# The graph stage by pairs of blocks: scores and attention in two-bank tiles

## The chip, the cores and the metric

The kernel runs on one core of one Trainium2 chip. The metric is the device time of one execution in microseconds; 2288.53 us is the median of three runs of the kernel before (2284.22 to 2291.29). Five engines work beside each other, each through its own queue in order: TensorE (matmuls, PE in the profile, its weight loads PEld), VectorE (DVE), ScalarE (ACT), GpSimd (POOL) and SyncE (SP), which issues the DMA transfers. Engines wait for one another by semaphores.

## The reference

The module is one decoder layer of three parts: a graph feature stage on `x`, a gated state-space scan, and a low-rank feed-forward part. Only the first concerns the change. For each batch of 512 nodes it orders the nodes along four space-filling curves, takes for each node and curve a window of ten neighbours, and runs a small attention over the ten:

```python
        def _get_graph_features(feats, inds_list, perm, W_lin, b_lin, k=K):
            ...
            for inds in inds_list:
                neigh = gather(feats, inds)
                gf = jnp.concatenate([jnp.broadcast_to(center, (B, N, k, C)), neigh - center], axis=-1)
                per_method.append(gf)
            allf = jnp.stack(per_method, axis=-1)
            allf = allf[..., perm]
            total = 2 * C * M_METHODS
            x = allf.reshape(B * N, k, total)
            x16 = x.astype(jnp.float16).astype(jnp.float32)
            ...
            scores = jnp.einsum('bihd,bjhd->bhij', qh, qh) / np.float32(np.sqrt(headdim))
            attn = jax.nn.softmax(scores, axis=-1)
            out = jnp.einsum('bhij,bjhd->bihd', attn, qh).reshape(B * N, k, total)
            fused = out @ W_lin.T + b_lin
            return fused.reshape(B, N, k, 64)
        ...
        g1 = _get_graph_features(f0, inds_list, perm1, W_lin1, b_lin1)
        h1 = jnp.einsum('oc,bnkc->bonk', W_conv1, g1)
        h1 = _lrelu(_instance_norm(h1, (2, 3)))
        feats1 = h1.max(axis=-1)
        g2 = _get_graph_features(feats1.transpose(0, 2, 1), inds_list, perm2, W_lin2, b_lin2)
        h2 = jnp.einsum('oc,bnkc->bonk', W_conv2, g2)
        h2 = _lrelu(_instance_norm(h2, (2, 3)))
        feats2 = h2.max(axis=-1)
```

## The kernel before

**Passes and blocks.** The sixteen batches are worked on in four groups of four. Each group goes through layer 1 (32 output channels, `npair` 1) and layer 2 (64, `npair` 2), which makes eight passes, in the order of `order` (L1026): layer 1 of groups 0 and 1, layer 2 of 0, layer 1 of 2, layer 2 of 1, layer 1 of 3, layer 2 of 2 and of 3. A pass is cut into 43 blocks of twelve nodes (`NGRP`, `NG`), so there are 344 blocks. The stage is written under a manual schedule: each engine's queue has the instructions in the order of the program text.

**One block.** `differences` (L782, GpSimd) subtracts centres from neighbours into `DD`, and every third block SyncE spreads a piece of three blocks from `DD` to `DX` (L821, four transfers). `scores` (L841, TensorE) lays a mask of large numbers into a PSUM tile `s` of one bank (L846) and adds sixteen small matmuls (L853). `greatest` (L860, VectorE) takes the negative maximum `c` of each row of scores. `expo` (L867) adds `c` to `s` by a matmul (L870, TensorE) and takes the exponential `e` (L875, ScalarE). `sums` (L878, VectorE) adds `e` up to `z`. `shares` (L885) has the reciprocal `rz` on VectorE (L888) and the product `EN` = `e` x `rz` on GpSimd (L890). `turn` (L892, VectorE) transposes 32 x 32 blocks of `EN` to `e2`. `mapped` (L899) projects the differences to `u` with 48 matmuls (L915, TensorE), which ScalarE copies to `us` (L920; one copy of 512 columns in layer 1, two in layer 2). `outputs` (L923) multiplies `us` with `e2` into `h` (L943, sixteen fp32 matmuls; four blocks share an `h` tile in layer 1, two in layer 2). When an `h` tile is full, `reduce` (L950, VectorE) adds the centre's share in layer 2 (`hs`, L960), takes the maximum over the ten neighbours (L966) and the statistics for the norm (L969); in layer 2 a part of it is put off by one block (`rest`, L981).

**Beside it.** `prep` (L627) is a generator that prepares the next pass: a layer norm or a transpose, one-hot matrices `oh` on VectorE (L751), and `place` (L701), twelve matmuls on TensorE that permute the features (L705). `steps` (L1045) moves it on by one or two steps for each block, or moves a tail, the closing work of the pass before. `rank_step` (L551) compares sort keys, one matmul (L540) and one ScalarE instruction (L541) at a time, to find the nodes' order for the later groups.

**The order.** The loop over blocks (L1074) starts each part at its own distance behind the newest block `it`: `scores`, `greatest` and `mapped` at 0, `expo`, `sums` and `shares` at 1, `turn` and `outputs` at 3, `reduce` at 4, `rest` at 5; `differences` runs six blocks ahead (`LEAD`). The score tiles have two buffers (`ps_s`, L611), `EN` has two tiles (L442). PSUM is full: two banks of `s`, two of `u`, two for `misc`, one for `pp`, one for `h`.

Of the kernel before, what the change touches and what calls it, by code (L numbers as in the profile page):

```python
# [18 lines left out]
P = 128  # L19
B = 16  # L20
C = 32
D = 512
# [355 lines left out]
def graph_part(nc, tc, cx, I, dram, id32, ones, xt, F0, layernorm_steps, rstd_steps, scan_input):  # L378
# [63 lines left out]
    EN = [keep.tile([P, NI, 32], F32, name=f"EN{k}") for k in range(2)]  # L442
# [32 lines left out]
    for t in (*DD, *EN):  # L475
        zero(t)
# [134 lines left out]
    ps_s = cx.enter_context(tc.tile_pool(name="gps_s", bufs=2, space=PSUM))  # L611
# [3 lines left out]
    def early_tile(n):  # L615
        if n % 2:
            return ps_s.tile([P, 512], F32, tag="s", name=f"kd{n}")
        return later_tile(n)
# [222 lines left out]
    def scores(at, gi):  # L841

        slot, c1 = at_piece(at, gi)
        d, dx = DD[slot], DX[slot]
        s = ps_s.tile([P, 512], F32, tag="s", name=f"s{at}_{gi}")[:, :NI * QB]
        nc.tensor.matmul(  # L846
            s, lhsT=mL.rearrange("p i q -> p (i q)"), rhs=mR, start=True, stop=False, skip_group_check=True
        )
        for j in range(NJ):
            c0 = c1 + j * QB  # L850
            for h in range(4):
                rh = slice(32 * h, 32 * h + 32)
                nc.tensor.matmul(  # L853
                    s[rh, j * 4 * QB:(j + 1) * 4 * QB].rearrange("p (b q) -> p b q", b=4),
                    lhsT=d[:, h, c0:c0 + 32], rhs=dx[:, h, :, c0:c0 + QB],
                    start=False, stop=(j == NJ - 1), skip_group_check=True,
                )
        live["s", at, gi] = s

    def greatest(at, gi):  # L860
        c = sm.tile([P, NI], BF16, tag="c", name=f"c{at}_{gi}")
        nc.vector.tensor_reduce(  # L862
            c, live["s", at, gi].rearrange("p (i q) -> p i q", q=QB), AX.X, ALU.max, negate=True
        )
        live["c", at, gi] = c

    def expo(at, gi):  # L867

        s, c = live.pop(("s", at, gi)), live.pop(("c", at, gi))
        nc.tensor.matmul(  # L870
            s, lhsT=idb, rhs=c.unsqueeze(2).to_broadcast([P, NI, QB]), start=False, stop=True,
            skip_group_check=True,
        )
        e = sm.tile([P, NI, QB], F32, tag="e1", name=f"e1{at}_{gi}", bufs=3)
        nc.scalar.activation(e, s.rearrange("p (i q) -> p i q", q=QB), AF.Exp, scale=smc)  # L875
        live["e1", at, gi] = e

    def sums(at, gi):  # L878

        e = live.pop(("e1", at, gi))  # L880
        z = sm.tile([P, NI], F32, tag="z", name=f"z{at}_{gi}")
        nc.vector.tensor_reduce(z, e, AX.X, ALU.add)  # L882
        live["z", at, gi] = e, z

    def shares(at, gi):  # L885
        e, z = live.pop(("z", at, gi))
        rz = sm.tile([P, NI], F32, tag="rz", name=f"rz{at}_{gi}")
        nc.vector.reciprocal(rz, z)  # L888
        en = EN[(at * NGRP + gi) % 2]
        nc.gpsimd.tensor_tensor(en[:, :, :QB], e, rz.unsqueeze(2).to_broadcast([P, NI, QB]), ALU.mult)  # L890

    def turn(at, gi):  # L892

        e = sm.tile([P, NI, 32], F32, tag="e2", name=f"e2{at}_{gi}", bufs=2)
        en = EN[(at * NGRP + gi) % 2]
        nc.vector.transpose(e.rearrange("p i q -> p (i q)"), en.rearrange("p i q -> p (i q)"))  # L896
        live["e2", at, gi] = e
# [25 lines left out]
    def outputs(at, gi):  # L923
        key, co, npair, WA, hc, per = state[at][:6]
        us, e = live.pop(("us", at, gi)), live.pop(("e2", at, gi))
        slot = gi % per
        if slot == 0:
            live["h", at] = ps_1.tile([P, npair, per * NQ], F32, tag="h", name=f"h{at}_{gi}")
            if npair == 1:

                f0 = gi * NG
                nn = min(f0 + per * NG, D) - f0
                nc.tensor.matmul(
                    live["h", at][:, 0, :nn * K].rearrange("p (n j) -> p n j", j=K), lhsT=id32,
                    rhs=hc[:, 0, f0:f0 + nn].unsqueeze(2).to_broadcast([P, nn, K]), start=True, stop=False,
                    skip_group_check=True,
                )
        h = live["h", at]
        for j in range(NJ):
            for b in range(4):  # L940
                pr, r = divmod(b * co, P)
                q0 = slot * NQ + j * QB
                nc.tensor.matmul(  # L943
                    h[r:r + co, pr, q0:q0 + QB], lhsT=us[:, j, b * co:(b + 1) * co],
                    rhs=e[:, 4 * j + b, :QB], start=npair > 1, stop=True, skip_group_check=True,
                )
        if slot == per - 1 or gi == NGRP - 1:
            live["full", at, gi] = h

    def reduce(at, gi):  # L950
# [14 lines left out]
        def greatest_of():  # L965
            nc.vector.tensor_reduce(mxo[:, :, f0:f0 + nn], hs, AX.X, ALU.max)  # L966

        def moments(pr):
            nc.vector.bn_stats(stats[:, pr, gi // per], hs[:, pr].rearrange("p n j -> p (n j)"))  # L969

        if npair == 1:
            greatest_of()
            moments(0)
        else:
            moments(0)
            live["rest", at] = lambda: (greatest_of(), moments(1))
        if gi == NGRP - 1:
            rest(at, gi)
            tails.append(end(at))

    def rest(at, gi):  # L981
        if ("rest", at) in live:
            live.pop(("rest", at))()
# [27 lines left out]
    def finish(g, F2):  # L1011
# [6 lines left out]
        n3 = wk.tile([P, D], F32, tag="n3", name=f"n3_{g}", bufs=1)  # L1018
# [55 lines left out]
    for it in range(len(blocks) + 5):  # L1074

        def do(step, lag):
            if 0 <= it - lag < len(blocks):
                step(*blocks[it - lag])

        at, gi = blocks[it] if it < len(blocks) else (len(order), 0)  # L1080
        if gi == 0 and it < len(blocks):
            begin(at)
        do(expo, 1)
        for oh, of in transfers:
            nc.scalar.dma_start(out=oh, in_=of)
        transfers.clear()
        do(turn, 3)
        do(scores, 0)
        do(rest, 5)
        do(reduce, 4)  # L1090
        if ranked[0] < wanted(at):
            rank_step(later_tile)
        do(greatest, 0)
        do(mapped, 0)
        do(sums, 1)
        if at + 1 == len(order) and gi == 4:
            tails.extend(scan_input(sm, junk(q), q) for q in range(NBG - 1))
        steps(at, gi)
        do(shares, 1)
        if ranked[0] < wanted(at) and (at == 0 or gi % 2):  # L1100
            rank_step(later_tile)
        do(outputs, 3)
        if at == 0 and gi < 8:
            rank_step(later_tile)
        if it + LEAD < len(blocks):
            to, g2 = blocks[it + LEAD]
            if g2 == 0:
                for _ in ahead[to][0]:
                    pass
            differences(to, g2)  # L1110
# [563 lines left out]
```

## Time and profile before

| what | us |
|---|---|
| median of three runs | 2288.53 (2284.22 to 2291.29) |
| the profiled execution, whole time | 2296.19 |
| the profiled execution, span from first to last instruction | 2294.1 |
| TensorE busy, in the whole span | 2099.9 (92%) |
| VectorE busy | 1796.4 (78%) |
| ScalarE busy | 1140.7 (50%) |
| GpSimd busy | 831.4 (36%) |
| L875, exponential, x344 | 227.3, mean 661 ns |
| L862, maximum, x344 | 220.8, mean 642 ns |
| L882, sum, x344 | 219.8, mean 639 ns |
| L888, reciprocal, x344 | 85.1, mean 248 ns |
| L890, product into EN, x344 | 342.3, mean 995 ns |
| L896, turn, x344 | 224.8, mean 654 ns |

The eight passes over the blocks lie between about 113 and 1296 us of the span; before them come the sort keys, after them the scan and the feed-forward part, which the change does not touch. "Busy" is time in which at least one instruction of the engine runs. Matmuls overlap in the array, so the busy time of a group of small matmuls is less than their count times the mean duration; the time from the start of one group to the start of the next is the surer reading. In a row of the order of time the columns are the start, the length, the engine, the line and the operation, output and inputs, and the count where several stand together; in brackets stands how long the engine was idle before and what ended the idle time. In a row of the groups come the busy time and the mean length of one instruction in ns, then the idle time before them and its releasers. The mean granted TensorE clock over the span is 0.978 of full speed.

### The profile page before, as it was taken

How to read it: one execution, taken by the hardware profiler on the slowest of the kernel's cores; microseconds unless marked ns; L12 is line 12 of the kernel's file. 1: busy time of each engine (PE TensorE's matmuls, PEld its weight loads, DVE VectorE, ACT ScalarE, POOL GpSimd, SP SyncE). 2: the span in 40 equal slices, each digit the busy share in tenths (PEclk: the TensorE clock that was granted, in tenths of full speed). 3: DMA queues.
4: the chain of work that ended last, by engine and by line, in shares of the span. 5: the costliest groups of instructions: out<-in, count | busy, mean ns of one | idle time of the engine just before them, and what ended most of it. 6: DMA issues, size and time to landing. Idle time of an engine off the chain costs nothing. (4 is left out here: it accounts for less than half of the span.)

```text
span 2294.1 us, 91947 instructions
## 1 busy us (share of the span) xinstructions
PE 2099.9 (92%) x40610; PEld 1274.3 (56%) x40610; DVE 1796.4 (78%) x3976; ACT 1140.7 (50%) x2073; POOL 831.4 (36%) x905
## 2 busy tenths in 40 slices
PE   5598899999999998889999789979999999999979
PEld 2255555776556775567777544446556465564422
DVE  8488897999989999989999854596876867765543
ACT  6686576556665554355555323343543534435321
POOL 2156656556565565665655300110211211111200
PEclk9899999999999999999999889989999999999989
DMA  1323232141232321423211122212131221311110
GB/s 47 80 61 81 53 76 64 45 93 45 57 79 47 77 57 41 98 47 73 61 36 37 28 73 71 69 58 88 36 99 51 60 88 41 94 52 55 38 37 19
DMA packets 121637, 138.18 MB, mean 60 GB/s; under 512 B 18398, under 2 KB 79506, under 8 KB 121154
## 3 DMA queue, kind: packets, MB, share of 16 engines
q1 hardware_dynamic: 121240, 132.32, 22.9%
q8 instruction: 319, 5.23, 1.0%
q14 instruction: 78, 0.64, 0.1%
HBM read 77.02 MB, written 12.85 MB: 39 GB/s over the span
## 5 line engine op out<-in xcount | busy, mean ns | idle before, releaser
L890 POOL TENSOR_TENSOR EN<-e,rz 128x480 f32<-128x480 f32 x344 | 342.3, 995 | 501.6 <-DVE rz L888 408.4
L915 PE MATMUL u<-WA,DD 128*32 128x128 bf16 (+1 forms) x16512 | 412.8, 247 | 21.1 <-issue 20.8
L920 ACT COPY us<-u 128x512 f32<-128x512 f32 x516 | 301.7, 586 | 157.1 <-PE u L915 140.7
L915 PEld LDWEIGHTS <-DD 128*32 128x32 f16 x16512 | 337.5, 97 | 55.3 <-issue 53.5
L875 ACT ACTIVATE e<-s,smc 128x480 f32<-128x480 f32 x344 | 227.3, 661 | 250.5 <-PE s L870 219.6
L811 POOL TENSOR_TENSOR DD<-fs,crep 128x480 f16<-128x480 f32 (+2 forms) x344 | 349.5, 1017 | 0.0
L943 PEld LDWEIGHTS h<-e,us 128*32 128x32 f32 (+1 forms) x11008 | 245.9, 125 | 133.0 <-issue 66.4
L943 PE MATMUL h<-e,us 128*32 128x30 f32 (+1 forms) x11008 | 278.8, 210 | 30.5 <-issue 12.8
L1377 POOL TENSOR_TENSOR ssq<-ssq,sq 128x512 f32<-128x512 f32 x56 | 79.6, 1421 | 582.3 <-ACT sq L1376 582.3
L862 DVE TENSOR_REDUCE c<-s 128x16 bf16<-128x480 f32 x344 | 220.8, 642 | 87.3 <-PE s L853 83.8
L1184 PE MATMUL ppg<-hT,wing 128*128 128x512 f32 x512 | 238.4, 609 | 0.0
L1184 PE MATMUL ppch<-hT,winch 128*128 128x512 f32 x512 | 230.9, 593 | 1.1 <-ACT gs L1272 1.1
L1197 DVE SCALAR_TENSOR_TENSOR cyh<-ppch,t_conv_w,cyh 128x496 f32<-128x496 f32 (+2 forms) x192 | 137.6, 717 | 119.8 <-ACT cyh L1191 115.3
L896 DVE STREAM_TRANSPOSE e<-EN 128x512 f32<-128x512 f32 x344 | 224.8, 654 | 0.0
L882 DVE TENSOR_REDUCE z<-e 128x16 f32<-128x480 f32 x344 | 219.8, 639 | 0.4 <-ACT e L875 0.4
L541 ACT ACTIVATE sgn<-kd 128x512 bf16<-128x512 f32 x256 | 153.1, 598 | 52.3 <-PE kd L540 49.3
L853 PEld LDWEIGHTS <-DD 128*32 128x32 f16 x5504 | 81.0, 96 | 159.1 <-issue 132.2
L751 DVE TENSOR_SCALAR oh<-it,rank 128x512 bf16<-128x512 f16 x512 | 155.9, 365 | 8.5 <-PE pp L705 8.5
L853 PE MATMUL s<-DX,DD 128*32 128x120 f16 x5504 | 142.4, 221 | 19.5 <-DMA DX<-DD 15.5
L1184 PEld LDWEIGHTS ppch<-hT,winch 128*128 128x128 f32 x512 | 94.3, 190 | 111.4 <-issue 101.7
L1184 PEld LDWEIGHTS ppg<-hT,wing 128*128 128x128 f32 x512 | 94.5, 192 | 101.8 <-issue 98.1
L870 PE MATMUL s<-c,idb 128*128 128x480 bf16 x344 | 130.3, 379 | 5.2 <-DVE c L862 2.7
(372 smaller groups left out, 3057.8 us busy)
## 6 DMA issues: line engine op xcount, KB each, us to landing
DX<-DD SPq DMA_DIRECT2D x456, 90.0 KB
wing<-in_in_proj SPq DMA_DIRECT2D x64, 256.0 KB
winch<-in_in_proj SPq DMA_DIRECT2D x64, 256.0 KB
wo<-in_out_proj SPq DMA_DIRECT2D x64, 256.0 KB
crep<-dC SPq DMA_DIRECT2D x128, 64.0 KB
dS<-so SPq DMA_DIRECT2D x32, 256.0 KB
fs<-dS SPq DMA_DIRECT2D x128, 64.0 KB
wincB<-in_in_proj SPq DMA_DIRECT2D x8, 256.0 KB
```

Of the source, the lines that this page charges most:

```text
L751: nc.vector.tensor_scalar(oh[:, j], it2, rank[:, c, m, 4 * g + b:4 * g + b + 1], None, ALU.is_equal)
L811: nc.gpsimd.tensor_tensor(d[:, :, m0 - n0:n1 - n0], win, crep[:, :, m0:n1].unsqueeze(3).to_broadcast([P, 4, n1 - m0, K]), ALU.subtract,)
L853: nc.tensor.matmul(s[rh, j * 4 * QB:(j + 1) * 4 * QB].rearrange("p (b q) -> p b q", b=4), lhsT=d[:, h, c0:c0 + 32], rhs=dx[:, h, :, c0:c0 ...
L862: nc.vector.tensor_reduce(c, live["s", at, gi].rearrange("p (i q) -> p i q", q=QB), AX.X, ALU.max, negate=True)
L875: nc.scalar.activation(e, s.rearrange("p (i q) -> p i q", q=QB), AF.Exp, scale=smc)
L882: nc.vector.tensor_reduce(z, e, AX.X, ALU.add)
L890: nc.gpsimd.tensor_tensor(en[:, :, :QB], e, rz.unsqueeze(2).to_broadcast([P, NI, QB]), ALU.mult)
L896: nc.vector.transpose(e.rearrange("p i q -> p (i q)"), en.rearrange("p i q -> p (i q)"))
L915: nc.tensor.matmul(u[rh, jj], lhsT=d[:, h, c0:c0 + 32], rhs=WA[k][:, h].rearrange("p b o -> p (b o)"), start=(jj == 0 and k == 0), stop=(k ...
L920: nc.scalar.copy(us[:, j - jj:j + 1], u)
L943: nc.tensor.matmul(h[r:r + co, pr, q0:q0 + QB], lhsT=us[:, j, b * co:(b + 1) * co], rhs=e[:, 4 * j + b, :QB], start=npair > 1, stop=True, ...
L1184: nc.tensor.matmul(pp, lhsT=w[:, k], rhs=hT[:, k], start=(k == 0), stop=(k == 3))
```

## The change

The loop goes over pairs of neighbouring blocks of a pass: 21 pairs and one single block, 22 for each pass, 176 in all. The score tile has two banks, one for each block of the pair, and one buffer in place of two; `EN` is one tile for two blocks. `greatest`, the exponential of `expo`, `sums`, the reciprocal, the product and `turn` are one instruction for a pair; `shares` is merged into `sums`. The matmuls of `scores`, `expo`, `mapped` and `outputs` are the same ones, block by block. `reduce` runs whole; `rest` is gone.

```diff
-    ps_s = cx.enter_context(tc.tile_pool(name="gps_s", bufs=2, space=PSUM))
+    ps_s = cx.enter_context(tc.tile_pool(name="gps_s", bufs=1, space=PSUM))
...
+    def scores(t):
+
+        at, gi, nb = pairs[t]
+        both = ps_s.tile([P, 2, 512], F32, tag="s", name=f"s{t}")
+        for i in range(nb):
...
+    def greatest(t):
+        nb = pairs[t][2]
+        c = sm.tile([P, 2, NI], BF16, tag="c", name=f"c{t}", bufs=2)[:, :nb]
+        nc.vector.tensor_reduce(c, live["s", t], AX.X, ALU.max, negate=True)
...
+    def expo(t):
...
+        for i in range(nb):
+            nc.tensor.matmul(
+                s[:, i], lhsT=idb, rhs=c[:, i].unsqueeze(2).to_broadcast([P, NI, QB]), start=False, stop=True,
+                skip_group_check=True,
+            )
+        e = sm.tile([P, 2, NI, QB], F32, tag="e1", name=f"e1{t}", bufs=2)[:, :nb]
+        nc.scalar.activation(
+            e.rearrange("p b i q -> p b (i q)"), s.rearrange("p b i q -> p b (i q)"), AF.Exp, scale=smc
         )
...
+    def sums(t):
...
+        nc.vector.tensor_reduce(z, e, AX.X, ALU.add)
+        rz = sm.tile([P, 2, NI], F32, tag="rz", name=f"rz{t}", bufs=2)[:, :nb]
+        nc.vector.reciprocal(rz, z)
+        nc.gpsimd.tensor_tensor(
+            EN[:, :nb, :, :QB], e, rz.unsqueeze(3).to_broadcast([P, nb, NI, QB]), ALU.mult
         )
...
+    def turn(t):
+
+        nb = pairs[t][2]
+        e = sm.tile([P, 2, NI, 32], F32, tag="e2", name=f"e2{t}", bufs=1)[:, :nb]
+        nc.vector.transpose(e.rearrange("p b i q -> p (b i q)"), EN[:, :nb].rearrange("p b i q -> p (b i q)"))
```

The loop, old and new:

```diff
-    for it in range(len(blocks) + 5):
...
-        do(expo, 1)
...
-        do(turn, 3)
-        do(scores, 0)
-        do(rest, 5)
-        do(reduce, 4)
...
-        do(greatest, 0)
-        do(mapped, 0)
-        do(sums, 1)
...
-        steps(at, gi)
-        do(shares, 1)
...
-        do(outputs, 3)
...
+    for t in range(len(pairs) + 3):
+        now = blocks_of(t)
...
+        before = blocks_of(t - 1)
+        if before:
+            expo(t - 1)
+        if now:
+            steps(*now[0])
+        for b in blocks_of(t - 2):
+            reduce(*b)
+        wide = now and state[at][2] > 1
+        for b in now[:1 if wide else 2]:
+            mapped(*b)
+        if before:
+            sums(t - 1)
+        if now:
+            scores(t)
+        if now and ranked[0] < wanted(at):
+            rank_step(later_tile)
+        if now:
+            greatest(t)
+        for b in now[1:] if wide else ():
+            mapped(*b)
+        for b in now:
+            if ranked[0] < wanted(at) and (at == 0 or b[1] % 2):
+                rank_step(later_tile)
...
+        for b in now[1:]:
+            steps(*b)
+        if before:
+            turn(t - 1)
...
+        for i, b in enumerate(before):
+            outputs(*b, live["e2", t - 1][:, i])
...
+        for _ in now:
+            if begun < len(blocks):
...
+                differences(to, g2)
+                begun += 1
```

`wide` is true in layer 2: there the second block's `mapped` comes after `greatest`. In layer 1 both blocks' `mapped` come before `scores`. One more edit lets the tile `n3` of a pass's closing work share a buffer with `lr`.

## The prediction

> **What bounds the kernel now.** I read the engine shares by stretch of time first, then the order of time on TensorE, then the place where the pipeline drains, then the groups by shape for the prices. The start of each L870 matmul (one for each of the 344 blocks, from the order of time) dates the eight passes of the graph stage: they begin at 113.1, 258.3, 399.1, 550.3, 699.3, 850.4, 996.4 and 1147.6 us, and the last ends near 1295.5. Passes 0, 1, 3, 5 are layer 1 and take 145.2 + 140.8 + 149.0 + 146.0 = 581.0 us; passes 2, 4, 6, 7 are layer 2 and take 151.2 + 151.1 + 151.2 + 147.9 = 601.4. So a pair of blocks takes 6.76 us in layer 1 and 6.99 in layer 2 (sum / 172 x 2). The view by stretches (columns: stretch, length, busy us of PE, PEld, DVE, ACT, POOL, granted clock, DMA):
>
> ```profile
> 500.00:530.00 30.00, 30.00 (x922) 23.81 (x910) 26.90 (x56) 17.45 (x29) 17.59 (x18) 1.00 0.31 67
> 580.00:640.00 60.00, 57.02 (x1749) 31.58 (x1745) 53.99 (x132) 39.98 (x89) 33.69 (x34) 1.00 0.28 64
> ```
>
> The first stretch lies in a layer 2 pass that prepares nothing: TensorE is never idle and VectorE has 10% left. The second is layer 1: both are near 90-95%, none full. TensorE's own order shows why layer 2 ticks so evenly:
>
> ```profile
> 531.24 0.38 PE L870 MATMUL s<-c,idb 128*128 128x480 bf16 x1
> 531.45 0.37 PE L846 MATMUL s<-mR,mL 128*128 128x480 bf16 x1
> 531.74 0.41 PE L853 MATMUL s<-DX,DD 128*32 128x120 f16 x16
> 531.97 1.49 PE L915 MATMUL u<-WA,DD 128*32 128x256 bf16 x48
> 533.39 1.12 PE L943 MATMUL h<-e,us 128*64 128x30 f32 x32
> 534.45 0.38 PE L870 MATMUL s<-c,idb 128*128 128x480 bf16 x1
> ```
>
> From start to start: 0.21 for the maximum's matmul, 0.29 + 0.23 scores, 1.42 for u, 1.06 for h, 3.21 us in all, and 3.86 with a `place` (0.75 for 12 matmuls, some of it overlapped). Nothing in it waits for the block's own softmax, because `turn` and `outputs` work three blocks behind `scores`. What that distance hides is seen only where the stage runs dry, at the last block:
>
> ```profile
> 1292.25 0.38 PE L870 MATMUL s<-c,idb 128*128 128x480 bf16 x1
> 1292.36 0.66 DVE L960 TENSOR_TENSOR hs<-h,hc 128x480 f32<-128x480 f32 x1 [0.29 <-PE h L943]
> 1292.72 0.66 ACT L875 ACTIVATE e<-s,smc 128x480 f32<-128x480 f32 x1 [0.83 <-POOL EN L890]
> 1293.41 0.65 DVE L882 TENSOR_REDUCE z<-e 128x16 f32<-128x480 f32 x1
> 1294.10 0.25 DVE L888 RECIPROCAL rz<-z 128x16 f32<-128x16 f32 x1
> 1294.53 0.99 POOL L890 TENSOR_TENSOR EN<-e,rz 128x480 f32<-128x480 f32 x1 [1.85 <-DVE rz L888]
> 1295.69 0.69 DVE L896 STREAM_TRANSPOSE e<-EN 128x512 f32<-128x512 f32 x1
> ```
>
> Each step starts 0.03 to 0.18 us after the one above it (hs apart): from the maximum's matmul to the end of the turn, 1296.38 - 1292.25 = **4.13 us for one block**.
>
> **The change, part by part.** (1) VectorE, ScalarE and GpSimd issue 176 instructions of each kind instead of 344. The rows that give an instruction's growth with its length:
>
> ```profile
> L811 POOL TENSOR_TENSOR DD<-fs,crep 128x480 f16<-128x480 f32 x328 | 338.1, 1031 | 0.0
> L811 POOL TENSOR_TENSOR DD<-fs,crep 128x320 f16<-128x320 f32 x8 | 6.0, 750 | 0.0
> L920 ACT COPY us<-u 128x512 f32<-128x512 f32 x516 | 301.7, 586 | 157.1 <-PE u L915 140.7
> L1465 ACT COPY ou<-po 128x256 f32<-128x256 f32 x6 | 2.2, 372 | 51.1 <-PE po L1450 51.1
> L966 DVE TENSOR_REDUCE mxo<-hs 128x48 f32<-128x480 f32 x84 | 51.0, 607 | 0.0
> 1298.86 0.30 DVE L966 TENSOR_REDUCE mxo<-hs 128x16 f32<-128x160 f32 x1
> ```
>
> GpSimd 1.76 ns for each element, ScalarE 0.84 (and 0.91 by the other half of L1465, 353 ns), VectorE 0.96. Another 480 elements then add 0.42 us to the exponential, 0.47 to a reduction, 0.84 to the multiply into EN; 512 add 0.50 to the turn, 16 add 0.02 to the reciprocal. VectorE is spared, for each pair, 0.17 twice, 0.23 and 0.15: 0.72 us, 168 x 0.72 = 121 us over the stage. In layer 2 this is worth nothing, since TensorE is full there; in layer 1 it could be worth some of it if nothing else changed. No row has these instructions at 960 elements: the bounds are no growth at all, and twice the present time (growth 0.66, 0.64, 0.25, 0.99, 0.65). I take the slopes, which are rows of the same engines.
>
> (2) The order changes, and this decides. In one pass of the new loop body come `expo(t-1)`, `sums(t-1)`, `turn(t-1)`, `outputs(t-1)`; TensorE runs its queue in order, so the next pair's `expo` stands behind `outputs(t-1)`, which waits for the turn, which waits for EN, the reciprocal, the sum and the exponential that this pass's own `expo` opened. The distance of three blocks is gone and the whole chain lies inside one pass. Its length: 4.13 for one block, + 0.21 for the second maximum's matmul, + 0.42 + 0.47 + 0.02 + 0.84 + 0.50 = **6.59 us**, + 0.06 to the first h matmul (1294.92 to 1294.98 in the drain), + the h matmuls of two blocks: 2 x 1.06 in layer 2, 2 x 0.39 in layer 1 (start of L943 to the next start, median of that layer). Layer 1: 7.43. Layer 2: 8.77.
>
> (3) What stands in the way on VectorE. `reduce(t-2)` is now whole and ahead of `sums`: in layer 2 hs, maximum and two statistics, 1.94 us in the drain (1296.30 to 1298.24), from 0.12 us after the pass begins, so the sum starts at 2.06 and not at 0.68 + 1.08 + 0.03 = 1.79: +0.27, 9.04 us. In layer 1 it comes every second pass with 0.62 + 0.65 us and fits before 1.79. The second `steps` stands between the maximum and the turn: where it makes four one-hots (1.14 to 1.49 us for x4 in the order of time) the turn is late by 0.5 to 0.9 us in layer 1, in the 8 of 22 passes that have two `place`, about +0.35 with the other preparation spread over all: 7.78 us. In layer 2 the same gives about +0.06: 9.1.
>
> (4) At no cost, with what hides it: TensorE's other work in a pass (both blocks' u and scores, and two `place`: 5.4 us in layer 2, 3.9 in layer 1) lies inside the 6 us for which it would wait anyway; without that cover it would cost its own length. `scores(t)` now waits for the exponential of the pair before (one two-bank tile, no second): that ends at 1.76 us, while u of the first block holds TensorE to 1.84 in layer 2, and to 1.76 with both blocks in layer 1; lacking that, up to 0.1. 21 rank steps move from each of passes 1 and 3 into 2 and 4 (0.3 us of TensorE, 0.8 of ScalarE apiece), inside the wait too; uncovered, 21 x 2 x 0.3 = 13 us. On GpSimd's queue two differences (2.06 us) stand behind EN and end 7.5 us into the pass, before the next EN; the DX transfers behind them on SP's queue keep their number (456) and are due a whole pass after their last column is written.
>
> **Sum.** 43 blocks are 21 pairs and one single, a single pass taking 4.13 + 0.06 + 0.39 = 4.6 in layer 1, 4.13 + 0.06 + 1.06 + 0.27 = 5.5 in layer 2. Layer 1: 4 x (21 x 7.78 + 4.6) = 672, +91. Layer 2: 4 x (21 x 9.1 + 5.5) = 786, +185. Together +276 on a profiled execution of 2296.19 us (span 2294.1), 2572; the median of the runs is 7.7 us lower, so **2564 us**.
>
> Two rules of the Trainium skill bear on this. The row for the multiply into EN says 1.76 ns for each element more. GPSIMD Engine Reference, section 3.1, puts a two-operand instruction at about 2.6 cycles for each element, 2.17 ns at its 1.2 GHz; by it EN grows by 1.04, and the estimate would be 168 x 0.20 = 34 us higher. The whole present instruction is 995 / 480 = 2.07 ns for each element with its fixed part, so the row is kept. The second speaks against the change: TensorE: Matmul & The Clock Gate, section "HAM oscillation", says that TensorE is throttled after idle gaps of over about 3.4 us. My gaps are 1.5 to 2.8 us, so by rule and row alike the clock stays; were it halved for all of TensorE's own 1.5 to 2.8 us in the chain, the estimate would be some 360 us higher.
>
> **Rivals.** *The long instructions are nearly free* (the other side; 4%). If they grew by nothing, the chain would be 4.40 + 0.78 = 5.2 us in layer 1 and TensorE would still set layer 2; layer 1 would gain the 0.72 for each pair, 84 x 0.72 = 60, so 2228. It decides once the growth of 2.25 us for each pair falls short by 276 / 168 = 1.64, under a third of it; the rows of two lengths, on three engines, speak against. *Late work in the chain* (19%): every instruction costs twice its old time (+0.94) and preparation delays the turn: layer 1 8.6, layer 2 10.0, with a clock below 1.00 as the 0.92 between 100 and 200 us: 4 x (21 x 8.6 + 4.6) + 4 x (21 x 10 + 5.5) = 1603, +421, 2709. For it: layer 1's intervals before scatter from 1.8 to 6.9 us. *Little in the way* (17%): EN grows by the 24-to-40-element rows of L800 (235 to 259 ns, 1.5 ns each, 0.72), the exponential by 0.36 (one element 203 ns against 586 for 512), and no delay from preparation: 7.2 and 8.75; 4 x (151.2 + 4.5) + 4 x (183.8 + 5.4) = 1380, +197, 2486.
>
> **How the numbers follow.** The forecast has 60%, its own range 2520 to 2610. The range of 8 in 10 runs from the low rival to short of the high one, 2475 to 2690. A difference under 0.3% (7 us) cannot be told from none; only the first rival gives faster or same.
>
> **What would show it.** Right: intervals of the two maximum's matmuls near 9 us in layer 2 and 7.5 to 8 in layer 1; TensorE idle 1 to 3 us in each pass ahead of h, released by the turn; VectorE's busy time lower by some 120 us; EN near 1.85 us, exponential 1.08, sum 1.11, turn 1.15. Wrong: h starting without a wait, layer 2 still at 6.4 a pair, or TensorE's clock far under 1.00 in the stage.

## The result, and the profile after

The changed kernel takes 2885.95 us, the median of four runs (2884.94 to 2894.72), beside 2289.91 us for the kernel before in the same four rounds: a ratio of 1.2615, 95% interval 1.258 to 1.2651. It is slower, as forecast, but by 596 us and not by 276; the time lies outside the forecast's range. The profiled execution has a span of 2884.6 us.

Nearly all of the loss, 584 us, is in the graph stage. Dated as before by the first L874 (the maximum's matmul; L870 before), the passes of layer 1 take 808 us (581 before, 672 forecast) and those of layer 2 958 us (601 before, 786 forecast). The view by stretches, with pass 1 (layer 1) and pass 6 (layer 2), in the columns explained in the prediction:

```profile
316.00:521.00 205.00, 145.80 (x4460) 89.37 (x4471) 132.69 (x190) 81.22 (x160) 83.51 (x74) 0.84 0.21 47
1398.00:1652.00 254.00, 194.12 (x4424) 139.36 (x4411) 164.22 (x254) 76.54 (x117) 83.72 (x74) 0.81 0.16 36
```

No engine is near full any more: TensorE is busy for 71% and 76% of the two stretches, VectorE for 65%. Both kinds of pass wait. The clock column is the second thing to see: 0.84 and 0.81, where the mean over the same stage was 0.99 before (0.92 to 1.00 in stretches of 100 us). What TensorE waits for is in its waits (us in total, times, longest):

```profile
PE h L947 <- DVE e L900: 377.9, 158, 5.3
```

That is the wait for the turn which the prediction placed there, in 158 of 176 passes of the loop body. The longest is 5.3 us; the forecast gaps were 1.5 to 2.8. The groups by shape show that the instructions themselves came out as costed:

```profile
L892 POOL TENSOR_TENSOR EN<-e,rz 128x960 f32<-128x960 f32 x168 | 303.4, 1806 | 1071.5 <-DVE rz L891 963.5 <-ACT us L924 83.7 <-DMA DX<-DD 24.3
L751 DVE TENSOR_SCALAR oh<-it,rank 128x512 bf16<-128x512 f16 x512 | 225.1, 496 | 60.0 <-PE pp L705 60.0
L900 DVE STREAM_TRANSPOSE e<-EN 128x1024 f32<-128x1024 f32 x168 | 207.5, 1235 | 30.9 <-POOL EN L892 30.7
L889 DVE TENSOR_REDUCE z<-e 128x32 f32<-128x960 f32 x168 | 192.9, 1148 | 104.4 <-ACT e L879 98.8 <-issue 2.5
L866 DVE TENSOR_REDUCE c<-s 128x32 bf16<-128x960 f32 x168 | 192.8, 1147 | 191.7 <-PE s L856 190.8
L879 ACT ACTIVATE e<-s,smc 128x960 f32<-128x960 f32 x168 | 178.2, 1061 | 727.6 <-PE s L874 512.7 <-issue 186.7 <-POOL DD L811 13.2
```

The product is 1.81 us (forecast 1.84), the exponential 1.06 (1.08), the sum 1.15 (1.11), the turn 1.24 (1.15). One row is out of line, and the change does not touch it: the one-hots, L751. The same 512 instructions of the same shape took less in the kernel before:

```profile
L751 DVE TENSOR_SCALAR oh<-it,rank 128x512 bf16<-128x512 f16 x512 | 155.9, 365 | 8.5 <-PE pp L705 8.5
```

Where their time went is seen in the order of time of one layer 2 pair with two `place` (TensorE's scores and ScalarE's copies left out):

```profile
1487.29 0.35 DVE L891 RECIPROCAL rz<-z 128x32 f32<-128x32 f32 x1
1487.56 1.09 DVE L866 TENSOR_REDUCE c<-s 128x32 bf16<-128x960 f32 x1
...
1487.81 1.81 POOL L892 TENSOR_TENSOR EN<-e,rz 128x960 f32<-128x960 f32 x1 [11.73 <-DVE rz L891]
1488.57 3.52 DVE L751 TENSOR_SCALAR oh<-it,rank 128x512 bf16<-128x512 f16 x4
1489.57 2.11 POOL L811 TENSOR_TENSOR DD<-fs,crep 128x480 f16<-128x480 f32 x2
1492.02 1.23 DVE L900 STREAM_TRANSPOSE e<-EN 128x1024 f32<-128x1024 f32 x1
...
1493.30 3.63 PE L947 MATMUL h<-e,us 128*64 128x30 f32 x64 [4.86 <-DVE e L900]
1496.87 0.98 PE L874 MATMUL s<-c,idb 128*128 128x480 bf16 x2
```

EN is ready at 1489.62, but VectorE starts the turn at 1492.02, 2.40 us later, because four one-hots of the second `steps` stand ahead of it and take 3.52 us. Three of the four, each by itself in a narrower view:

```profile
1488.57 1.20 DVE L751 TENSOR_SCALAR oh<-it,rank 128x512 bf16<-128x512 f16 x1
...
1490.72 1.11 DVE L751 TENSOR_SCALAR oh<-it,rank 128x512 bf16<-128x512 f16 x1
...
1491.76 0.34 DVE L751 TENSOR_SCALAR oh<-it,rank 128x512 bf16<-128x512 f16 x1
```

The first three end when GpSimd's running instruction ends (EN at 1489.62, then each of the two differences, some 1.03 us apart up to 1491.68); the fourth, with GpSimd idle, takes 0.34. Over the whole execution, the 376 one-hots beside which no GpSimd instruction ran have a median of 0.34 us, and the 136 that started while one ran a median of 1.11.

The h matmuls in this pair are the second loss: 3.63 us for 64, where 1.99 is the normal distance from their start to the next. They ran at half clock.

The mean over the 168 pairs, cut at the steps of the chain (the base is the median of the fastest tenth of the pairs):

| stretch of a pair, us | base, layer 1 / 2 | mean, layer 1 / 2 | excess x 84 pairs each, together |
|---|---|---|---|
| first L874 to the sum | 1.76 / 2.00 | 2.03 / 2.27 | 45 |
| sum to the product | 1.71 / 1.70 | 1.72 / 1.71 | 2 |
| product to the turn | 1.84 / 1.84 | 3.38 / 3.21 | 244 |
| turn to the h matmuls | 1.29 / 1.29 | 1.35 / 1.32 | 8 |
| h matmuls to the next L874 | 0.69 / 1.99 | 0.82 / 2.57 | 60 |

The base adds up to 7.29 and 8.82 us, beside the forecast chain of 7.43 and 9.04. The excess is 359 us; the forecast had allowed 64 of it (7.78 and 9.1 us less the base).

The one-hots are not all of the third row. At most 512 x (0.496 - 0.341) = 79 of its 244 us are length that GpSimd adds to them. Another part has no one-hot in it, as in this layer 1 pair (other rows left out):

```profile
454.05 2.75 PE L919 MATMUL u<-WA,DD 128*32 128x128 bf16 x96
...
455.93 1.81 POOL L892 TENSOR_TENSOR EN<-e,rz 128x960 f32<-128x960 f32 x1 [5.78 <-DVE rz L891]
...
457.69 0.40 PE L856 MATMUL s<-DX,DD 128*32 128x120 f16 x16
...
458.14 1.16 DVE L866 TENSOR_REDUCE c<-s 128x32 bf16<-128x960 f32 x1 [2.38 <-PE s L856]
...
459.21 1.23 DVE L900 STREAM_TRANSPOSE e<-EN 128x1024 f32<-128x1024 f32 x1
```

EN is ready at 457.74, but the maximum, which stands ahead of the turn on VectorE, has waited for the scores, and these stand behind both blocks' u on TensorE. Read pair by pair from the order of time, the 244 us are 70 for a maximum that ends after EN is ready (94 of the 168 pairs), 121 for the one-hots that follow it (62 pairs, at their plain length and with the hold), and 53 for other preparation on VectorE, casts and norms (39 pairs).

### The profile page after: what moved, and what is told of

It is laid out like the page before. It is cut to its first block, busy times and chain, and to the rows that moved or that the text cites. A ratio compares the mean times of both kernels' runs of the same rounds, so it can differ in the third digit from the quotient of the medians.

```text
span 2884.6 us, 90521 instructions
## 1 busy us (share of the span) xinstructions
PE 2313.7 (80%) x40526; PEld 1399.0 (48%) x40610; DVE 1893.1 (66%) x3304; ACT 1094.3 (38%) x1905; POOL 808.4 (28%) x736
## 5 line engine op out<-in xcount | busy, mean ns | idle before, releaser
L892 POOL TENSOR_TENSOR EN<-e,rz 128x960 f32<-128x960 f32 (+1 forms) x176 | 311.3, 1769 | 1113.8 <-DVE rz L891 1005.8
L947 PEld LDWEIGHTS h<-e,us 128*32 128x32 f32 (+1 forms) x11008 | 280.0, 147 | 488.8 <-DVE e L900 456.8
L919 PE MATMUL u<-WA,DD 128*32 128x128 bf16 (+1 forms) x16512 | 484.9, 283 | 29.3 <-issue 18.7
L879 ACT ACTIVATE e<-s,smc 128x960 f32<-128x960 f32 (+1 forms) x176 | 183.5, 1043 | 776.7 <-PE s L874 561.8
L866 DVE TENSOR_REDUCE c<-s 128x32 bf16<-128x960 f32 (+1 forms) x176 | 197.6, 1123 | 192.8 <-PE s L856 191.9
L889 DVE TENSOR_REDUCE z<-e 128x32 f32<-128x960 f32 (+1 forms) x176 | 198.0, 1125 | 113.7 <-ACT e L879 108.0
L751 DVE TENSOR_SCALAR oh<-it,rank 128x512 bf16<-128x512 f16 x512 | 225.1, 496 | 60.0 <-PE pp L705 60.0
L900 DVE STREAM_TRANSPOSE e<-EN 128x1024 f32<-128x1024 f32 (+1 forms) x176 | 213.2, 1211 | 32.1 <-POOL EN L892 31.9
L964 DVE TENSOR_TENSOR hs<-h,hc 128x480 f32<-128x480 f32 x88 | 56.4, 641 | 170.6 <-PE h L947 170.6
L849 PE MATMUL s<-mR,mL 128*128 128x480 bf16 x344 | 137.8, 400 | 0.4 <-ACT e L879 0.4
```

The costliest lines, as they stand in the source:

```text
L751: nc.vector.tensor_scalar(oh[:, j], it2, rank[:, c, m, 4 * g + b:4 * g + b + 1], None, ALU.is_equal)
L866: nc.vector.tensor_reduce(c, live["s", t], AX.X, ALU.max, negate=True)
L879: nc.scalar.activation(e.rearrange("p b i q -> p b (i q)"), s.rearrange("p b i q -> p b (i q)"), AF.Exp, scale=smc)
L892: nc.gpsimd.tensor_tensor(EN[:, :nb, :, :QB], e, rz.unsqueeze(3).to_broadcast([P, nb, NI, QB]), ALU.mult)
L900: nc.vector.transpose(e.rearrange("p b i q -> p (b i q)"), EN[:, :nb].rearrange("p b i q -> p (b i q)"))
L919: nc.tensor.matmul(u[rh, jj], lhsT=d[:, h, c0:c0 + 32], rhs=WA[k][:, h].rearrange("p b o -> p (b o)"), start=(jj == 0 and k == 0), stop=(k ...
```

## The experiments

Each is a single run beside the kernel before on the same chip (2288 to 2293 us), but for the one that is said to be measured in three rounds.

**The second steps behind the turn.** Only the place in VectorE's order changes.

```diff
-        for b in now[1:]:
-            steps(*b)
         if before:
             turn(t - 1)
+        for b in now[1:]:
+            steps(*b)
```

> The second steps of a pass is moved behind the turn, all else as in the changed kernel. Theory H (VectorE's one-hots and small operations are held by GpSimd's product and differences, and the turn stands behind them): the turn starts 1.85 to 2.2 us after the product's start in pairs with a place, where it now starts after 4.1 to 4.4; 63 such pairs x 2.3 = 145 us less, up to 50 more from pairs with other preparation, up to 60 given back where the one-hots now delay the next sum: 2720 to 2800 us. Rival C (only TensorE's clock was missed): the time stays at 2886, within 20.

Measured: 2660.43 us, 226 less than the changed kernel. That is better than H's range by 60. The product-to-turn mean falls to 2.01 us in layer 1 and 1.98 in layer 2, an excess of 26 us in place of 244; what is left is all maxima that end late. One pair with two `place` in the order of time (VectorE, GpSimd and the TensorE rows of the chain):

```profile
1321.61 2.01 POOL L811 TENSOR_TENSOR DD<-fs,crep 128x480 f16<-128x480 f32 x2
1321.68 1.25 DVE L900 STREAM_TRANSPOSE e<-EN 128x1024 f32<-128x1024 f32 x1 [1.00 <-POOL EN L892]
1322.85 2.23 DVE L751 TENSOR_SCALAR oh<-it,rank 128x512 bf16<-128x512 f16 x6
1322.98 3.63 PE L947 MATMUL h<-e,us 128*64 128x30 f32 x64 [2.58 <-DVE e L900]
1326.55 0.98 PE L874 MATMUL s<-c,idb 128*128 128x480 bf16 x2
1327.46 1.49 PE L705 MATMUL pp<-oh,F 128*32 128x512 bf16 x12
...
1328.98 0.62 DVE L751 TENSOR_SCALAR oh<-it,rank 128x512 bf16<-128x512 f16 x2 [3.91 <-PE pp L705]
...
1331.40 1.14 DVE L889 TENSOR_REDUCE z<-e 128x32 f32<-128x960 f32 x1
```

The turn, which is not held, now runs beside the differences, and six one-hots take 2.23 us in all. What remains is seen in the same rows: h at half clock (3.63), and one-hots that wait for a `place` behind the maximum's matmuls, so that the sum starts 4.85 us after L874 and not 2.00.

**The gap on TensorE filled.** Eight matmuls of 480 columns into a tile that nobody reads stand ahead of h, where TensorE waits for the turn. They add work and no result.

```diff
         if before:
             turn(t - 1)
+        if now and before:
+            idle = later_tile(1000 + t)
+            for k in range(8):
+                nc.tensor.matmul(idle[:, :NI * QB], lhsT=idb, rhs=mR, start=True, stop=True)
```

> The changed kernel with eight matmuls of 480 columns into an unused tile put on TensorE ahead of the h matmuls of each pair, in the time in which it waits for the turn. Theory C (the granted clock falls because TensorE idles for 2 to 4 us in each pass): the clock between 120 and 1890 us rises from 0.8-0.88 to over 0.92, the h matmuls of layer 2 fall from a mean of 2.54 us for a pair towards 2.1, and the time falls by 60 to 110: 2775 to 2830 us. Rival (the clock costs nothing, or does not follow the idle time): 2886 or up to 100 more for the added matmuls.

Measured: 2821.38 us, 65 less than without the extra work: theory C, within its range. The same stretch of the stage in the changed kernel, and in this one:

```profile
400.00:800.00 400.00, 303.81 (x7953) 205.39 (x7985) 266.18 (x414) 154.62 (x292) 151.26 (x136) 0.85 0.19 43
```

```profile
400.00:800.00 400.00, 348.37 (x8849) 221.15 (x8872) 286.95 (x439) 161.74 (x311) 160.16 (x142) 0.98 0.20 45
```

The clock goes from 0.85 to 0.98 and the h stretch of layer 2 from 2.57 to 2.16 us, while the turn is as late as before in the pairs with four one-hots (medians of 4.25 and 4.21 us after the product, in place of 4.42 and 4.21). So the clock is a loss by itself. In the table above its terms are L874 to the exponential (0.84 and 0.90 us in place of 0.67, 34 us of the first row) and the 60 of the last row, together 94; with the fill they are 32. Two more terms of the 65 partly cancel: the mean from product to turn falls by 34 us, because the maxima are late by 29 us in all in place of 70, and the fill costs 24 between turn and h.

**Both edits in one.** The two diffs above together: turn, then the eight matmuls, then the second steps.

> Both single edits in one: the second steps behind the turn, and eight matmuls of 480 columns into a tile that nobody reads, ahead of h. The first alone gave 2660 us (226 less than the changed kernel), the second 2821 (65 less). Theory: late one-hots and the lowered clock are two separate losses on the same chain, so that what is left is the chain of the prediction, 7.4 us a pair in layer 1 and 8.8 in layer 2, with some waits of the first steps: 2560 to 2620 us, clock 0.95 or more in the stage. Rival (the clock fell only because the turn was late; with the turn on time the fill has nothing to mend): 2645 to 2680, as without the fill.

Measured: 2679.39 us, clock 0.97: outside the theory's range and just inside the rival's, but not for the rival's reason, since the fill does mend something. The h stretch of layer 2 does fall, to 2.06 us from 2.33 with the first edit alone, and layer 2's pairs without a `place` to a median of 8.83. The fill has a price of its own here: turn to h is now 2.02 us in layer 1 and 1.61 in layer 2 in the mean, against 1.29, because the turn comes early and the eight matmuls with the `place` outlast the wait. Against the first edit alone, the stretches ahead of the turn and behind the start of h gain 62 us, and turn to h loses 83; the run took 19 more. This run does not tell what the kernel would take at full clock with nothing in the gap.

**The one-hot in another form.** The order is that of the changed kernel. Only the instruction differs.

```diff
-                            oh[:, j], it2, rank[...], None, ALU.is_equal
+                            oh[:, j], it2, rank[...], None, ALU.is_equal,
+                            ALU.add, accum_out=hits,
```

> The changed kernel with its order untouched; only the one-hot's instruction also writes out the sum of its row, which nobody reads. Theory H with the rule of the Trainium skill, page SBUF — State Buffer, section Who interferes with whom (a VectorE operation in a mode of two ports is blocked for as long as a GpSimd instruction runs; the form that writes its accumulator is none of these): the one-hots take one fixed time, near 0.6 us, whether GpSimd runs or not; four of them then end 2.4 us after the product starts in place of 4.1, the turn starts 2.3 to 2.7 us after the product in the pairs with a place, and the time falls by 60 to 150 us to 2735 to 2825, although each one-hot alone is longer. Rival (the one-hots wait for something else: TensorE's release of their tile, or any VectorE work beside GpSimd is slowed): their length still varies with GpSimd's work, the turn is as late as before, and the time is 2886 or more.

Measured: 2989.6 us, 104 more than the changed kernel; the theory's time is missed by 165. But the rows answer the question about the hold:

```profile
L752 DVE TENSOR_SCALAR_CACHE_REDUCE oh<-it,rank 128x512 bf16<-128x512 f16 x512 | 378.8, 740 | 62.1 <-PE pp L706 39.7 <-DVE oh L752 2.6
L752 DVE DVE_READ_ACCUMULATOR oh<-it,rank 128x1 f32 x512 | 42.4, 83 | 0.0
```

All 512 take 0.70 to 0.75 us: those that met a GpSimd instruction (176) have a median of 0.745, those that did not (336) 0.746. The dependence on GpSimd is gone, so it belonged to the form of the instruction and not to the tile or to TensorE. The time rose because this form has its own length, 0.74 with 0.08 for its second part, where I had assumed 0.6; the one-hots of the changed kernel, held ones included, have a mean of 0.50. The turn stays late, 3.53 and 3.34 us after the product in the mean.

**The hold on single blocks.** The kernel before with one line moved.

```diff
-        steps(at, gi)
         do(shares, 1)
+        steps(at, gi)
```

> The kernel before, single blocks, with nothing moved but the steps of the preparation: behind the reciprocal and the product instead of ahead of them, so that the one-hots fall beside GpSimd's product. Theory H (a one-hot on VectorE is held until the running GpSimd instruction ends): more than 200 of the 512 one-hots take 0.6 us or more, where 38 did, VectorE's order slips in the blocks that prepare, and the time rises by 20 to 120 us, to 2310 to 2410. Rival (one-hots are late in the changed kernel for its own reasons, and hold nothing here): the one-hots stay at 0.34 us and the time stays within 15 us of 2291.

Measured: 2476.32 us, 188 more than the kernel before; more than H's range, far from the rival. 214 of the 512 one-hots take over 0.6 us, where 25 did in the kernel before (the expectation said 38). Two of its groups, and the order of time of one block:

```profile
L890 POOL TENSOR_TENSOR EN<-e,rz 128x480 f32<-128x480 f32 x344 | 361.3, 1050 | 653.3 <-DVE rz L888 278.6 <-DVE oh L751 272.0 <-DMA DX<-DD 26.7
L751 DVE TENSOR_SCALAR oh<-it,rank 128x512 bf16<-128x512 f16 x512 | 297.9, 643 | 8.6 <-PE pp L705 8.6
```

```profile
171.52 0.25 DVE L888 RECIPROCAL rz<-z 128x16 f32<-128x16 f32 x1
...
171.69 2.57 DVE L751 TENSOR_SCALAR oh<-it,rank 128x512 bf16<-128x512 f16 x4
...
171.94 1.12 POOL L890 TENSOR_TENSOR EN<-e,rz 128x480 f32<-128x480 f32 x1 [2.33 <-DVE oh L751]
```

The hold needs no pairs: it needs a one-hot that starts while a GpSimd instruction runs. The 214 that did took 1.1 us; the 232 that overlapped one but had started before it took 0.35. GpSimd pays too, by less: the product's length goes from 0.995 to 1.05 us in the mean, and in this block to 1.12.

**The outputs one pass later.** Pairs stay; `outputs` goes behind `expo` of the next pass, so that TensorE no longer waits for a turn that this pass's own `expo` opened. `mapped` of both blocks goes between `scores` and `greatest`, `reduce` behind the turn, and the second `steps` behind it too, as in the first experiment.

```diff
         if before:
             expo(t - 1)
+        for i, b in enumerate(older):
+            outputs(*b, live["e2", t - 2][:, i])
...
         if before:
             turn(t - 1)
-        for i, b in enumerate(before):
-            outputs(*b, live["e2", t - 1][:, i])
+        for b in older:
+            reduce(*b)
+        for b in now[1:]:
+            steps(*b)
```

> The pairs as in the changed kernel, but the outputs of a pair stand one pass later, right behind the next pair's maximum matmul, and reduce stands behind the turn. Theory O (the order, which closes the whole chain inside one pass, makes the stage slow, not the long instructions): TensorE no longer waits for the turn; layer 2 6.8 to 7.3 us for a pair, layer 1 5.8 to 8, the time 2240 to 2400 us. Rival (the long instructions or the single two-bank score tile cost the time): over 2600.

Measured: 2495.24 us, 391 less than the changed kernel, 165 less than with the second steps alone behind the turn, and 95 above the top of the expected range. Layer 2 without preparation ticks at 6.67 us a pair. Layer 1 alternates between about 5.3 and 9.0 us: in every second pair the first h matmul, L937, waits for the statistics, which this order puts behind the turn:

```profile
788.95 1.25 DVE L900 STREAM_TRANSPOSE e<-EN 128x1024 f32<-128x1024 f32 x1 [0.99 <-POOL EN L892]
790.11 0.62 DVE L969 TENSOR_REDUCE mxo<-h 128x48 f32<-128x480 f32 x1
790.66 0.65 DVE L971 BATCH_NORM_STATS2 stats<-h 128x6 f32<-128x480 f32 x1
...
791.45 1.32 PE L937 MATMUL h<-hc,id 128*128 128x480 f32 x2 [2.19 <-DVE stats L971]
```

**The same, with the h tile freed earlier.** Layer 1's reduction, and layer 2's addition into `hs`, go between the maximum and the turn; the rest of layer 2's reduction stays behind it.

```diff
         if now:
             greatest(t)
+        for b in older:
+            reduce(*b)
...
         if before:
             turn(t - 1)
         for b in older:
-            reduce(*b)
+            rest(*b)
```

> The pairs with the outputs one pass later, as in the run that took 2495 us, and the reduction placed so that TensorE finds its h tile free: layer 1's whole reduction, and layer 2's addition into hs, stand between the maximum and the turn; the rest of layer 2's reduction stands behind the turn. Theory O (what is lost to the kernel before is order, here the wait of every second pair's first h matmul for the statistics): layer 1's pairs no longer alternate between 5.3 and 9.0 us, the passes of layer 1 fall from about 170 to 145 to 155 us, layer 2 stays at 6.5 to 6.9 a pair, and the time is 2270 to 2400 us. Rival (long instructions cost whatever the order): the passes keep 165 us or more, and the time stays at 2450 or above.

Measured in three rounds: 2396.68 us (2395.0 to 2402.87), 1.0482 of the kernel before, interval 1.0465 to 1.05: at the top of O's range. The same place in a layer 1 pass:

```profile
732.86 0.66 DVE L982 BATCH_NORM_STATS2 stats<-h 128x6 f32<-128x480 f32 x1
...
733.43 1.23 DVE L900 STREAM_TRANSPOSE e<-EN 128x1024 f32<-128x1024 f32 x1
733.66 1.04 PE L937 MATMUL h<-hc,id 128*128 128x480 f32 x2
```

L937 no longer waits here. Layer 1 takes 610 us (581 in the kernel before) and layer 2 664 (601), so most of what is left is in layer 2, whose pairs take 7.6 us in the mean and not 6.5 to 6.9; the clock is 0.973. Late in a pass, with nothing to prepare, a pair takes 5.9 us in layer 1, where the kernel before takes 6.3, and 6.7 in layer 2, where it takes 6.4; with two `place`, layer 2 takes 8.5 against 7.7. So 489 of the 596 us come back with the long instructions left as they are, 226 of them already by the place of the second steps alone. One wait is new beside the kernel before, TensorE's for the exponential before it may write the one score tile again:

```profile
PE s L849 <- ACT e L879: 31.0, 30, 2.0
```

I did not find where all of the last 107 go, and no version here beats the kernel before.

**The order alone, on single blocks.** The kernel before, with `turn` and `outputs` at distance 1 behind `shares`, at the end of the pass, `reduce` at 2 and `rest` at 3.

```diff
-        do(turn, 3)
...
         do(shares, 1)
+        do(turn, 1)
...
-        do(outputs, 3)
+        do(outputs, 1)
```

> The kernel before, single blocks, with turn and outputs moved from three blocks behind to one, at the end of the same pass. Theory O: each block takes the chain of 4.6 us in layer 1 and 5.5 in layer 2, 172 x 10.1 = 1737 against 1182 us, so 2840 us, and up to 3000 with a lower clock and with one-hots held by GpSimd. Rival (pairing costs, the order does not): under 2400.

Measured: 3269.65 us, 977 more than the kernel before and more than expected. TensorE's wait for the turn, and a stretch of the stage:

```profile
PE h L943 <- DVE e L896: 723.1, 332, 4.6
```

```profile
400.00:800.00 400.00, 263.56 (x6527) 166.03 (x6546) 206.89 (x466) 136.36 (x273) 124.17 (x134) 0.80 0.16 37
```

332 of 344 blocks wait, 2.18 us each, and the clock is at 0.80. In about this order pairs are better than single blocks by 384 us, since a chain of one block is paid 344 times and one of two blocks 176 times. The order that the tiles of two blocks came with is most of the loss. That the tiles cost nothing themselves is not shown: the best version with them is still 107 us behind, 31 of it perhaps the wait for the one score tile.

## Why the prediction was right in direction and wrong in size

**The chain in one pass: right.** Part (2) said that expo, sum, product, turn and h would lie one behind another, 7.43 and 8.77 us, 9.04 in layer 2 with the reduction. The fastest tenth of the pairs shows 7.3 and 8.8. The two runs with the outputs one pass later confirm that the order is the main loss (264 us between the first experiment and the better of them, at the same place of the steps, with `mapped` and `reduce` moved too), and the one on single blocks that it does not depend on the long instructions.

**The lengths: nearly right.** Exponential, sum and product are within 0.04 us; the turn and the reciprocal are 0.09 and 0.08 longer than the slopes gave. GpSimd's product grew by 1.69 ns for each element more, nearer the row's 1.76 than the 2.17 that the prediction set beside it. VectorE's busy time was to fall by some 120 us. Its four kinds of instruction fell by only 80 (maximum 23, sum 22, reciprocal 24, turn 12), the one-hots rose by 67, and its busy time as a whole rose from 1796.4 to 1893.1 us.

**The step that failed** is in part (3): "where it makes four one-hots (1.14 to 1.49 us for x4 in the order of time) the turn is late by 0.5 to 0.9 us in layer 1, in the 8 of 22 passes that have two `place`, about +0.35 with the other preparation spread over all", and 0.06 in layer 2. It was measured at 1.54 us a pair in layer 1 and 1.37 in layer 2: 244 us in place of about 34. The mechanism was right, the second `steps` ahead of the turn; its size was not, in three terms.

- The one-hots, 121 us. They stood ahead of the turn in about as many layer 1 pairs as forecast (35 of 84), but the turn was late by 2.6 us there, not by 0.5 to 0.9, and by 2.4 us in 27 pairs of layer 2. I took their length from the order of time of before, where they mostly ran with GpSimd idle. In the new order they can start in the first half of a product twice as long, with two differences right behind it, so that up to three of four are held. The upper value, 1.49 us for four, already held one such case, and I read it as scatter. The hold is at most 79 us of the 121; the rest is their plain length, which the prediction expected the wait for EN to cover in part.
- The other preparation in the second `steps`, 53 us.
- The maximum, 70 us. Part (3) put its own lateness at nothing. It ended after EN was ready in 94 of the 168 pairs, since its scores came late on TensorE.

The runs show the step and the hold: with the second `steps` behind the turn 218 of the 244 us go, 44 of the 70 for late maxima among them; another form of the instruction is not held; and single blocks suffer the same when their one-hots meet the product. The split into three terms is read from one trace; no run takes them apart.

Behind the hold stands a rule that I did not weigh. The Trainium skill, page SBUF — State Buffer, section "Who interferes with whom", says that a VectorE instruction in a mode of two ports, `tensor_scalar` among them, is blocked for the whole of a running GpSimd instruction, and that the form which also writes its accumulator is not. Rows of 0.34 and 1.11 us in one kernel, and 0.74 in every case for the other form, agree with both halves.

**The clock: wrong.** The prediction held that with gaps of 1.5 to 2.8 us "the clock stays". It fell to 0.81 to 0.91 in the passes, and the terms that show it add up to 94 us, beside its share in the late maxima. Some gaps were longer than worked out, since the turn was late: 27 of the 207 stretches over 0.3 us without a matmul in the stage exceed 3.4 us, the longest 5.4. But such gaps are not needed: in the run with the order alone on single blocks only 9 of 204 such stretches, between 120 and 1250 us, exceed 3.4 us, the median is 2.1, and the clock is 0.80 throughout. The Trainium skill, TensorE: Matmul & The Clock Gate, section "HAM oscillation", names the gaps over 3.4 us; the rows here show a lowered clock with regular gaps of 2 to 3.

The clock records in the traces say more. They change only at multiples of 3.41 us, between full and half. In the graph stages of the ten profiled runs, all 301 stretches of 3.41 us at full clock in which TensorE was busy, by the profile, for less than 40% were followed by half clock; of the 2621 with 70% or more one was, and of the 671 between them 190. A gap of 2.1 us in such a stretch leaves 38%. Three stretches in a row of the run on single blocks show it:

```profile
208.01:211.42 3.41, 1.32 (x81) 0.92 (x73) 1.83 (x4) 1.87 (x5) 1.98 (x2) 1.00 0.00 0
211.42:214.83 3.41, 3.41 (x89) 1.84 (x75) 2.70 (x5) 1.35 (x3) 0.05 (x1) 0.50 0.02 5
214.83:218.25 3.42, 2.95 (x70) 1.30 (x66) 1.03 (x2) 1.84 (x4) 1.93 (x2) 1.00 0.06 14
```

TensorE is busy for 1.32 of 3.41 us in the first, has half clock in the second and is full there, and full clock again in the third.

**At no cost: only in part.** `place` and u cost nothing on TensorE itself where it waits. But part (4) looked at TensorE's wait alone: `scores` stand behind them, and with late scores the maximum and the turn on VectorE are late, the 70 us above. The first steps cost something too: their one-hots can wait for a `place` behind the maximum's matmuls and hold up the sum, as in the pair shown at 1326.55. In the first row of the table at most 11 us are left for it once the clock's 34 are taken out; it is small.

**The sum.** 276 us were forecast. To these come 244 + 94 + 11 + 8 + 2 = 359, less the 64 that the forecast had allowed, 295; with 276 that is 571 of 596. The remaining 25 I did not take apart; 13 of them lie in the stage (584 less 571), where the eight single blocks and the changes of pass are not among the 168 pairs of the table. "Late work in the chain" was the rival on the right side, with preparation ahead of the turn and a clock below 1.00, but at 8.6 and 10.0 us a pair, where 9.3 and 11.1 were measured.

## What to carry to other kernels

Putting work of several blocks into one instruction pays only if the distance between the stages stays: at about equal order pairs saved 384 us here, and the lost distance cost more. When an instruction is moved, look at what other engines run at its new place, and not only at its length at the old one; a group whose lengths scatter (0.34 and 1.11 us in one row) depends on something that the move may change. Look also at what stands ahead of it in its queue, and what that waits for. And when a wait on TensorE appears in every pass, count a lower clock into the estimate for the matmuls behind it: here the busy share of each 3.41 us decided, not the longest gap.

## What was not expected of the hardware

- A one-hot of 512 columns on VectorE takes 0.34 us alone; if it starts while a GpSimd instruction runs, it ends with that one: 1.11 us behind differences of 1.03 us each. If it starts first, it is not held. The turn and the maxima are not held either: the turn takes 1.24 us in the median beside GpSimd and 1.23 without, the maximum 1.16 in all 124 cases beside it.
- The form with an accumulator costs 0.74 + 0.08 us for the same 512 columns, and is not held.
- TensorE's clock fell to 0.80 with gaps whose median is 2.1 us: it halves for the next 3.41 us after a stretch of that length with TensorE busy for less than 40%, in 301 cases of 301. It came back from 0.85 to 0.98 with matmuls into an unused tile; the time fell with it by 65 us, although TensorE had more to do.
